# A conv–Mamba–attention hybrid on one core: the scan's exponentials from PSUM to SBUF, with a sibling's other settings

## The chip, the core and the metric

One core of a Trainium2 chip runs the whole program in one launch. The metric is the device time of an execution in microseconds (us). The engines are TensorE (PE in the profile; PEld is its loading of weights), VectorE (DVE), ScalarE (ACT), GpSimd (POOL) and SyncE (SP), which issues nearly all transfers between main memory and SBUF. Matrix products land in PSUM, eight banks of 128 x 512 numbers of 32 bits; GpSimd's operands here are all in SBUF.

## What is computed

The input is x, 8 images of 384 channels x 32 x 32 pixels, all in 32-bit floats. Layer 0 norms each pixel over its channels, runs two selective scans (Mamba) over the 1024 pixels, one in each direction, adds a local branch (a 3x3 depthwise convolution, a sigmoid, times the normed input), and adds all that to x. Layer 1 is causal attention over the 1024 tokens and a feed-forward block whose weights are Kronecker products. What matters here is the scan, cut from the reference:

```python
delta = jax.nn.softplus(jnp.einsum('blr,dr->bld', dt, dt_proj_w) + dt_proj_b)
deltaA = jnp.exp(delta[..., None] * A)
deltaBu = (delta * u)[..., None] * Bm[:, :, None, :]
def step(h, inp):
    dA, dBu, c = inp
    h = dA * h + dBu
    return (h, jnp.einsum('bdn,bn->bd', h, c))
...
y = ys.transpose(1, 0, 2) + u * D_param
y = y * silu(z)
```

There are 384 channels with 16 states each, so 6144 recurrences over 1024 steps, for each image and direction.

## The kernel before

**The scan.** A tile of 128 partitions holds 32 channels x 4 states. For an image the kernel works through four (direction, half) steps of 512 pixels (`STEPS`, line 33), and for each through 12 units: 3 blocks of 128 channels (`cc`) by 4 groups of states (`g`). A unit has four tiles of 128 x 512, handled as a "quad" 128 x 2048. In `scan` (line 974) a unit does this:

- SP has put delta times u, spread over the states, into a quad (`du`, from the pool of five `hs` quads), delta into `dl`, B into `br` and C into `cr`.
- GpSimd multiplies the quad `du` by `br` into the quad `hs` (line 1049); this is B u. The very first quad of the program is done by VectorE in four pieces (line 1047).
- ScalarE takes the exponential of `dl` into `da`, once for each of the four tiles. `da` is a PSUM tile, one of five banks (`DAS`, line 1054).
- VectorE runs `tensor_tensor_scan` on each tile (line 1061): h = da * h + B u. In "split" units the result goes back into `da` (PSUM), ScalarE copies its last column into `carry` if the other half of the image needs it, and VectorE multiplies `da` by `cr` into `hs`, one tile at a time (line 1068). In the other units (`POOL_C`, 4 of 12, and `POOL_END`, 5 of 12, in the last image) the scan's result goes into `hs`, and GpSimd multiplies the whole quad by `cr` (line 1075).
- TensorE sums over the states by four matmuls with `sel` into the one PSUM bank `y`, which also receives the D term (`ud` by `ddiag`, once for both directions of a half, their sum made by GpSimd in `prepare`, line 904) and, for the second direction, the first one's result (`y_t`).

Of the eight PSUM banks `y` has one, `da` five, and all other products ("side work") share two, `w`. At the very end of the program side work gets `da` banks in turn with `w` (`FREE`).

**The side work.** Arrival and norm (`norm_in`), gate (`raw_gate`), the convolutions, the rates (`prepare`), the local branch (`local`, line 832), the projection (`project`, 1103), attention (1152) and the feed-forward block (1269) of an image run beside the scans of that image, the one before or the one after. `local` adds x on GpSimd; `feed_forward` multiplies the normed tokens by `c2` on GpSimd and sums groups on VectorE (`xr`). All weights stay in SBUF from the start on.

**What sets the order.** No loop issues instructions directly. `Plan` records every operation with a due time in units of the scan, written by hand in tables (`FIRST`, `OTHERS`, `LAYER1`, `SCAN`, ...) and spread over the pieces of a stage. `Plan.order` (line 301) then plays all engines with a cost for each operation, binds tiles to buffers, and fixes each engine's queue. Each engine runs its queue in that order, and an instruction waits for the data and buffers it needs. The planner also puts filler matmuls into TensorE's idle time (`y<-zero,ident` in the profile). All operations are issued on line 460, so the profile is read by tile names, not by lines.

Of the kernel before, what the change touches and what calls it, by code (L numbers as in the profile page):

```python
# [30 lines left out]
P = 128  # L31
HB = 512
# [3 lines left out]
TMP, SIDE = 5, 4  # L36
REPS = 4
RUSH = 3.54
START, LATER = -40.0, -8.0
# [3 lines left out]
FIRST = (1.62, 3.96, 10.3, 14.48, 18.18, 21.76)  # L43
SECOND = (22.86, 0.54)
OTHERS = (4.13, 9.04, 14.9, 17.86, 22.66, 25.08, 29.09, 34.25, 42.87, 49.8)
BURST = 8.07
PROJECT = 1.35
LAYER1 = (39.85, 51.29, 60.87, 72.21, 83.5)
LAYER1_6 = (43.34, 50.01, 57.44, 69.38, 72.99)
LAYER1_7 = (39.84, 42.87, 51.35, 57.52, 62.56, 71.14, 71.63, 74.06, 81.9)  # L50
HASTE = 26.32
FREE = ["w", "da", "w", "da"]
EXPS = -0.17
SCAN = (-1.49, -1.1, -0.44, -0.43, -0.36, 0.14, 0.08, 1.19, 0.79)
DU_AHEAD = 3.37
DL_AHEAD = 3.22
DLS = 5
DAS = 5
# [22 lines left out]
class Plan:  # L81
# [9 lines left out]
    LOOSE = ("w", "tmp", "side")  # L91
    HURRY = 8.29
    PATIENCE = 1.77
    TAIL = dict(tensor=0.21, vector=0.117, scalar=0.14, gpsimd=0.1, sync=0.1)
    RAW = 0.07
    NEXT = 0.01
    TURN = 0.1
# [5 lines left out]
    KEEP = 0.65  # L103
# [197 lines left out]
    def order(self):  # L301
# [73 lines left out]
        while issued < total:  # L375
            best = None
            for e in engines:
                ts = [(at(op), op) for op in cand[e]]
                ts = [(t, op) for t, op in ts if t is not None]
                if not ts:  # L380
                    continue
                now = max(clock[e], min(t for t, _ in ts))
                if best is None or now < best[0]:
                    best = (now, e, ts)
# [3 lines left out]
            op = min((op for t, op in ts if t <= now), key=lambda op: op.rank)  # L388
# [14 lines left out]
            if e == "tensor" and self.nothing and now > clock[e]:  # L403

                y = [name for name in left_y if name in self.slot and users[name]]
                begun = bool(y) and left_y[y[0]] not in (0, all_y[y[0]])
                if begun or not y and max([last[n] for n in left_y if n in last], default=0.0) < clock[e]:
                    made = self._fill(max(array) + self.TURN * (form != (P, P)), now, begun)
                    started += made
                    if made:  # L410
                        array = [self.ran[-1][1]] * 4
                        form = P, P
                        now = max(now, array[0] + self.TURN * (op.form != form))
# [50 lines left out]
def conv_attn_kernel(  # L464
# [44 lines left out]
    ps_b = ctx.enter_context(tc.tile_pool(name="ps_b", bufs=1, space=bass.MemoryType.PSUM))  # L509
# [3 lines left out]
    rota = ["w"]  # L513

    def bank():
        rota.append(rota.pop(0))
        if rota[-1] == "w":
            return plan.tile(ps_w, [P, HB], "w", 8 - 1 - DAS)
        return plan.tile(ps_b, [P, HB], "da", DAS)

# [30 lines left out]
    win = load(in_wT[:, :C].rearrange("(cc p) e -> p cc e", p=P), [P, NC, C], "win")  # L551
# [25 lines left out]
    taps, flat = (plan.tile(l0, [P, HB], "side", SIDE)[: C // BC, :P] for _ in range(2))  # L577
# [21 lines left out]
    none = plan.tile(l0, [P, HB], "side", SIDE)[:, : NC * (WP + 1)]  # L599
# [13 lines left out]
    whose = plan.tile(l0, [P, HB], "side", SIDE)[:CG, :P]  # L613
# [23 lines left out]
    for cc in range(NC):  # L637
# [17 lines left out]
        plan.tile(l0, [P, HB], "side", SIDE)[: C // BC, : KW * KW * BC] for _ in range(2)  # L655
# [21 lines left out]
    wz = load(in_wT[:, C:].rearrange("(cc p) e -> p cc e", p=P), [P, NC, C], "wz")  # L677
    wout = load(out_wT.rearrange("(cc p) e -> p cc e", p=P), [P, NC, C], "wout")
    wvs = load(wv.rearrange("(cc p) e -> p cc e", p=P), [P, NC, C], "wvs")

    fc1s = weight([P, NF, P], "fc1s")
    for to in range(NG):
        for g in range(NG):
            plan.sync.dma_start(
                fc1s[to * NJ : (to + 1) * NJ, g::NG], fc1[g * NJ : (g + 1) * NJ]
            )
    fc1f = fc1s.rearrange("p f e -> p (f e)")
    plan.gpsimd.tensor_scalar_mul(fc1f, fc1f, 1.0 / NG)
# [20 lines left out]
    every = weight([P, NJ], "every")  # L709
    plan.vector.tensor_add(every, ident[:, :NJ], ident[:, NJ : 2 * NJ])  # L710
    for g in range(2, NG):
        plan.vector.tensor_add(every, every, ident[:, g * NJ : (g + 1) * NJ])
    emat = weight([P, NJ, NI], "emat")
    plan.vector.tensor_mul(
        emat,
        every.unsqueeze(2).to_broadcast([P, NJ, NI]),
        cp2.unsqueeze(1).to_broadcast([P, NJ, NI]),
    )
    emat = emat.rearrange("p j i -> p (j i)")
    plan.tile(ps_y, [P, HB], "y")  # L720
# [18 lines left out]
    def norm_in(b, h):  # L739
        xt = load_x(b, h)  # L740
        yield
# [36 lines left out]
    def raw_gate(b, h):  # L778

        xn, z = xn_t[b, h], plan.tile(dram, [P, NC, HB], "zr", 4)  # L780
# [51 lines left out]
    def local(b, h):  # L832

        cols = slice(h * HB, (h + 1) * HB)
# [4 lines left out]
        for cc in range(NC):  # L839
            xt = tmp()  # L840
            plan.sync.dma_start(xt, xv[b, :, cc, cols])
# [5 lines left out]
            plan.gpsimd.tensor_add(xt, xt, sg[:, cc])  # L847
            plan.sync.dma_start(lx[cc * P : (cc + 1) * P], xt)
# [55 lines left out]
    def prepare(b, steps):  # L904
# [45 lines left out]
        ud = ud_t[b, steps[0]] = plan.tile(dram, [C, HB], "ud", 4)  # L950
        for cc in range(NC):
            u = uc_t[b, steps[0]][:, cc]
            for si in steps[1:]:
                both = tmp()
                plan.gpsimd.tensor_add(both, u, uc_t[b, si][:, cc])
                u = both
            plan.sync.dma_start(ud[cc * P : (cc + 1) * P], u)
# [13 lines left out]
    def side():  # L971
        return plan.tile(l0, [P, HB], "side", SIDE)

    def scan(b, si, lo=0, hi=HB):
# [5 lines left out]
        ud = ud_t.get((b, si))  # L980
# [25 lines left out]
        for k in range(n_u):  # L1006
            cc, g = divmod(k, SG)
            t = t0 + f * k
            if g == 0:
# [19 lines left out]
                parts = []  # L1029
                if ud is not None:  # L1030
                    parts.append((ddiag[:, cc], ud[cc * P : (cc + 1) * P, lo:hi]))
# [6 lines left out]
                y = plan.tile(ps_y, [P, HB], "y")[:, :n]  # L1038
# [12 lines left out]
            for i in range(NQ):  # L1051
                j = cc * NQ + i
                plan.due, plan.rush = t + f * SCAN[1 + i], EXPS
                da = plan.tile(ps_b, [P, HB], "da", DAS)[:, :n]
                plan.scalar.activation(da, dl[i], AF.Exp, scale=nega[:, j, g : g + 1])
                plan.due, plan.rush = t + f * SCAN[5] * i, 0.0
                o, a, r = hs[:, i], da, da if split else hs[:, i]
                if d:
                    o, a, r = o[:, ::-1], a[:, ::-1], r[:, ::-1]
                init = carry[:, k, i : i + 1] if restore or lo else 0.0  # L1060
                plan.vector.tensor_tensor_scan(r, a, o, init, ALU.mult, ALU.add)
                if split:
                    if save:
                        plan.due, plan.rush = t + f * SCAN[5] * (i + 0.1), RUSH
                        plan.scalar.copy(carry[:, k, i : i + 1], da[:, 0:1] if d else da[:, n - 1 :])
                        plan.rush = 0.0
                    plan.due = t + f * (SCAN[5] * i + SCAN[6])
                    plan.vector.tensor_mul(hs[:, i], da, cr[g])
            if not split:
                if save:  # L1070
                    plan.due, plan.rush = t + f * 0.6, RUSH
                    plan.scalar.copy(carry[:, k], hs[:, :, 0 if d else n - 1])
                    plan.rush = 0.0
                plan.due = t + f * SCAN[8]
                plan.gpsimd.tensor_mul(hs, hs, cr[g].unsqueeze(1).to_broadcast([P, NQ, n]))
# [27 lines left out]
    def project(b, h, t1, lo=0, hi=HB):  # L1103

        yz = [yz_t[b, h, lo, cc] for cc in range(NC)]
        lx = []
        for cc in range(NC):
            lx.append(tmp()[:, : hi - lo])
            plan.sync.dma_start(lx[cc], lx_t[b, h][cc * P : (cc + 1) * P, lo:hi])
        yield  # L1110
        for i in range((hi - lo) // P):
# [7 lines left out]
            for cc in range(NC):  # L1119
                plan.tensor.matmul(  # L1120
                    po[:, cc * P : (cc + 1) * P], lx[cc][:, cols], ident,
                    start=False, stop=cc == NC - 1, is_transpose=True, skip_group_check=True,
                )
# [4 lines left out]
    def token_norm(t1, ti0, nt):  # L1128
# [9 lines left out]
        plan.gpsimd.tensor_scalar_mul(nrm[:, 1], mv[:, :, 0], -1.0)  # L1138
        plan.gpsimd.tensor_mul(nrm[:, 1], nrm[:, 1], nrm[:, 0])
# [12 lines left out]
    def attention(b, t1, t0, n, end=False):  # L1152
# [15 lines left out]
        for i in range(nt):  # L1168
            xt = normed(t1, tile0, nrm, i)
            pt = bank()  # L1170
            for cc in range(NC):
                plan.tensor.transpose(
                    pt[:, cc * P : (cc + 1) * P], xt[:, cc * P : (cc + 1) * P], ident
                )
            plan.scalar.copy(
# [18 lines left out]

        kp = turned(wks, "kp")
# [73 lines left out]
    def feed_forward(b, t1, t0, n, direct=False):  # L1269
# [4 lines left out]
        xr = plan.tile(l1, [P, NT, NJ], "xr")  # L1274
        for i in range(nt):
            xt = normed(t1, tile0, nrm, i).rearrange("p (j i) -> p j i", i=NI)
            plan.gpsimd.tensor_mul(xt, xt, c2.unsqueeze(1).to_broadcast([P, NJ, NI]))
            plan.vector.reduce_sum(xr[:, i], xt, axis=AX.X)
            yield
        px = bank()[:, :n]  # L1280
        for i in range(nt):
            for g in range(NG):
                plan.tensor.matmul(
                    px[g * NJ : (g + 1) * NJ, i * P : (i + 1) * P], xr[:, i], ident,
                    start=True, stop=True, skip_group_check=True,
# [6 lines left out]
        for f0 in range(0, NF, NF // 2):  # L1292
            gl = plan.tile(l1, [P, NF // 2, HB], "gl")[:, :, :n]
            for k in range(0, NF // 2, 2):
                ph = [bank()[:, :n], bank()[:, :n]]
                for i in range(2):
                    plan.tensor.matmul(ph[i], fc1s[:, f0 + k + i], xrT, start=True, stop=True)
# [10 lines left out]
            po = bank()[:, :n]  # L1308
            for k in range(NF // 2):
# [3 lines left out]
                    start=k < NG, stop=k >= NF // 2 - NG, skip_group_check=True,  # L1313
                )
            if f0 == 0:
                plan.scalar.copy(ob, po)
            else:
                plan.vector.tensor_add(ob, po, ob)
# [41 lines left out]
    for b in range(NB):  # L1360
# [21 lines left out]
        else:  # L1382
            first, rate = SECOND if b == 1 else (B - PER, 1.0)
            v = [first + rate * u for u in OTHERS]
# [12 lines left out]
        for si, (d, h) in enumerate(STEPS):  # L1397

            parts = ((0, HQ), (HQ, HB)) if last and si == 3 else ((0, HB),)
            for lo, hi in parts:  # L1400
                e = B + (si + hi / HB) * NU * SG
                scan(b, si, lo, hi)
                if si >= 2:
                    rota[:] = FREE if last and si == 3 and hi == HB else ["w"]
# [93 lines left out]
```

## Time and profile before

| | us |
|---|---|
| median of 3 runs | 3051.7 (3050.02 to 3054.4) |
| the profiled execution, its own time | 3053.55 |
| its span, first to last instruction | 3051.8 |
| TensorE / VectorE / ScalarE / GpSimd busy | 2698.0 / 2700.1 / 2175.5 / 2686.7 |
| mean granted TensorE clock | 0.969 of full |
| moved by DMA | 632.77 MB, mean 207 GB/s |

Everything below is read from one profiled execution. A group is all instructions of one engine with the same output and inputs by name ("hs<-da,cr" is hs written from da and cr); with it come the count, the busy time, the mean duration of one, and the time the engine sat idle just before, with what it waited for. An instruction's duration includes its start-up, so instructions back to back start closer together than one lasts.

### The profile page before, as it was taken

What the parts mean: (1) busy time and instruction counts of PE and PEld (TensorE: products, weight loads), DVE (VectorE), ACT (ScalarE), POOL (GpSimd) and SP (SyncE); (2) the same over time, 40 slices, a digit from 0 to 9 for tenths busy, and PEclk for the clock granted to TensorE, in tenths of its full rate; (3) what the DMA queues carried; (4) which work ended last, traced back from release to release, by engine and by line L of the source; (5) the groups of instructions that cost most, each with busy time, mean ns of one, the idle gap of its engine ahead of it and who ended that gap; (6) DMA issues with size and microseconds to landing.
All of it is one profiled execution on the core that took longest, in us unless ns stands there. A gap on an engine that the chain in (4) does not pass through costs nothing. (4 is left out here: it accounts for less than half of the span.)

```text
span 3051.8 us, 39365 instructions
## 1 busy us (share of the span) xinstructions
PE 2698.0 (88%) x12021; PEld 1188.4 (39%) x12021; DVE 2700.1 (88%) x3514; ACT 2175.5 (71%) x3928; POOL 2686.7 (88%) x914
## 2 busy tenths in 40 slices
PE   8877897998999899988889898999989998988889
PEld 3322343343443434333343434434343433434445
DVE  3898938998899989998999979999899989999982
ACT  3765656778778786867768686787868687676774
POOL 2999868989898999989898999989998999999960
PEclk9988998999999999999999999999999999999999
DMA  7786776567766677666766667556775577533410
GB/s 249 242 275 215 230 263 221 183 225 251 240 202 200 221 259 229 201 205 223 244 194 204 225 217 251 198 193 224 258 231 186 201 242 254 168 131 121 149 54 17
DMA packets 345836, 632.77 MB, mean 207 GB/s; under 512 B 42544, under 2 KB 57208, under 8 KB 345624
## 3 DMA queue, kind: packets, MB, share of 16 engines
q1 hardware_dynamic: 345496, 630.14, 62.5%
q8 instruction: 95, 1.56, 0.2%
q14 instruction: 117, 0.96, 0.1%
q0 software_dynamic: 128, 0.11, 0.0%
HBM read 475.71 MB, written 154.38 MB: 206 GB/s over the span
## 5 line engine op out<-in xcount | busy, mean ns | idle before, releaser
L460 POOL TENSOR_TENSOR hs<-hs,br 128x2048 f32<-128x2048 f32 (+1 forms) x395 | 1739.0, 4418 | 167.8 <-PE y L460 85.2
L460 ACT ACTIVATE da<-dl,nega 128x512 f32<-128x512 f32 (+1 forms) x1584 | 1036.3, 676 | 402.5 <-DVE hs L460 386.4
L460 DVE TENSOR_TENSOR hs<-da,cr 128x512 f32<-128x512 f32 (+1 forms) x1036 | 656.8, 666 | 27.7 <-ACT carry L460 27.0
L460 DVE TENSOR_TENSOR_SCAN da<-da,carry,hs 128x512 f32<-128x512 f32 (+1 forms) x532 | 628.4, 1220 | 38.9 <-POOL hs L460 24.7
L460 DVE TENSOR_TENSOR_SCAN da<-da,hs 128x512 f32<-128x512 f32 x504 | 598.0, 1218 | 64.9 <-ACT da L460 48.4
L460 POOL TENSOR_TENSOR hs<-hs,cr 128x2048 f32<-128x2048 f32 (+1 forms) x137 | 600.1, 4380 | 54.4 <-DVE hs L460 31.4
L460 PE MATMUL y<-hs,sel 128*32 128x512 f32 (+1 forms) x3168 | 467.9, 616 | 97.3 <-POOL hs L460 81.1
L460 PE MATMUL y<-zero,ident 128*128 128x256 f32 x1470 | 387.9, 397 | 0.0
L460 DVE TENSOR_TENSOR_SCAN hs<-da,carry,hs 128x512 f32<-128x512 f32 (+1 forms) x284 | 324.1, 1192 | 13.0 <-ACT da L460 7.7
L460 PEld LDWEIGHTS y<-zero,ident 128*128 128x128 f32 x1470 | 271.2, 195 | 149.3 <-issue 119.1
L460 DVE TENSOR_TENSOR_SCAN hs<-da,hs 128x512 f32<-128x512 f32 x264 | 308.3, 1208 | 20.4 <-ACT da L460 19.4
L460 PEld LDWEIGHTS y<-hs,sel 128*32 128x32 f32 x3168 | 93.4, 111 | 337.7 <-issue 128.5
L458 ACT ACT_TABLE_LOAD x164 | 210.4, 1283 | 2.9
L460 PE MATMUL w<-q,fc1s 128*128 128x512 f32 (+1 forms) x396 | 198.2, 617 | 15.0 <-ACT gl L460 7.4
L460 PE MATMUL w<-v,p 128*128 128x384 f32 x562 | 200.8, 504 | 8.4 <-ACT p L460 4.7
L460 ACT COPY carry<-da 128x1 f32<-128x1 f32 x532 | 81.0, 163 | 170.8 <-DVE da L460 168.8
L460 PE MATMUL w<-rep,cit 96*32 96x512 f32 x1152 | 153.0, 606 | 9.4 <-DMA rep<-xq 7.3
L460 ACT COPY gl<-w 128x512 f32<-128x512 f32 (+2 forms) x254 | 137.5, 551 | 12.8 <-PE w L460 11.7
L460 PE MATMUL w<-wout,side 128*128 128x384 f32 x378 | 137.9, 503 | 7.9 <-ACT t L460 3.6
L460 PEld LDWEIGHTS w<-v,p 128*128 128x128 f32 x562 | 105.1, 194 | 90.9 <-ACT p L460 19.7
L460 PE MATMUL w<-xn,wz 128*128 128x512 f32 x288 | 132.8, 601 | 3.9 <-ACT tmp L460 3.4
L460 PE MATMUL w<-xn,win 128*128 128x512 f32 x288 | 130.7, 600 | 1.9 <-ACT tmp L460 0.9
(188 smaller groups left out, 3421.2 us busy)
## 6 DMA issues: line engine op xcount, KB each, us to landing
dl<-dd SPq DMA_DIRECT2D x372, 256.0 KB, 4.0
hs<-db SPq DMA_DIRECT2D x372, 256.0 KB, 4.5
rep<-up SPq DMA_DIRECT2D x180, 257.5 KB, 4.3
rep<-xq SPq DMA_DIRECT2D x192, 222.4 KB, 4.9
br<-bd SPq DMA_DIRECT2D x124, 256.0 KB, 4.6
cr<-bd SPq DMA_DIRECT2D x124, 256.0 KB, 4.3
tmp<-in_x_dram SPq DMA_DIRECT2D x96, 256.0 KB, 4.6
dd<-tmp SPq DMA_DIRECT2D x96, 256.0 KB, 3.4
```

Of the source, the lines that this page charges most:

```text
L458: self.nc.scalar.preload_act_table_set(table)
L460: op.call(*args, **{k: self._bind(v) for k, v in op.kw.items()})
```

## The change

- **da in SBUF.** `da` becomes seven SBUF tiles. PSUM is split anew: six banks for side work, two for `y`. The rotation of side work into `da` banks goes.
- **Scans.** Every scan writes over B u in the quad `hs`. `carry` is copied once per quad. In split units VectorE multiplies the whole quad by `cr` at once (128 x 2048). Which units are split stays.
- **The sibling's other settings.** `tmp` and `side` become one pool of eight. The four large weights share two SBUF tiles (`heavy`) and are loaded again for each image (`wvs` for each attention part). The D term is added for each direction, without GpSimd's sum. `local` no longer adds x; `project` adds it by a second transposing matmul. `nrm` is finished by one VectorE instruction instead of two of GpSimd. The feed-forward block transposes the normed tokens and applies `c2` by a matmul (`c2s`) instead of GpSimd and VectorE; `fc1s` is a quarter of the size, used by 32 rows at a time; the second half's sum into `ob` is a matmul.
- **Planner.** Other due times, per image in part; a limit on how far ahead of the oldest candidate an operation may be taken (`SIGHT`); a penalty for a switch of ScalarE's table (`YIELD`).

```diff
-TMP, SIDE = 5, 4
+TMP = 8
+YS = 2
+WTS = 2
-DAS = 5
+DAS = 7
...
     def bank():
-        rota.append(rota.pop(0))
-        if rota[-1] == "w":
-            return plan.tile(ps_w, [P, HB], "w", 8 - 1 - DAS)
-        return plan.tile(ps_b, [P, HB], "da", DAS)
+        return plan.tile(ps_w, [P, HB], "w", 8 - YS)
...
+    def heavy(nm, key):
+        if (nm, key) not in big:
+            src = dict(win=in_wT[:, :C], wz=in_wT[:, C:], wout=out_wT, wvs=wv)[nm]
+            t = big[nm, key] = plan.tile(const, [P, NC, C], "wt", WTS)
+            plan.sync.dma_start(t, src.rearrange("(cc p) e -> p cc e", p=P))
+        return big[nm, key]
...
-            plan.gpsimd.tensor_add(xt, xt, sg[:, cc])
-            plan.sync.dma_start(lx[cc * P : (cc + 1) * P], xt)
+            plan.sync.dma_start(lx[cc * P : (cc + 1) * P], sg[:, cc])
...
-        ud = ud_t[b, steps[0]] = plan.tile(dram, [C, HB], "ud", 4)
-        for cc in range(NC):
-            u = uc_t[b, steps[0]][:, cc]
-            for si in steps[1:]:
-                both = tmp()
-                plan.gpsimd.tensor_add(both, u, uc_t[b, si][:, cc])
-                u = both
-            plan.sync.dma_start(ud[cc * P : (cc + 1) * P], u)
+        for si in steps:
+            ud = ud_t[b, si] = plan.tile(dram, [C, HB], "ud", 8)
+            for cc in range(NC):
+                plan.sync.dma_start(ud[cc * P : (cc + 1) * P], uc_t[b, si][:, cc])
...
-                y = plan.tile(ps_y, [P, HB], "y")[:, :n]
+                y = plan.tile(ps_y, [P, HB], "y", YS)[:, :n]
...
-                da = plan.tile(ps_b, [P, HB], "da", DAS)[:, :n]
+                da = plan.tile(l0, [P, HB], "da", DAS)[:, :n]
                 plan.scalar.activation(da, dl[i], AF.Exp, scale=nega[:, j, g : g + 1])
                 plan.due, plan.rush = t + f * SCAN[5] * i, 0.0
-                o, a, r = hs[:, i], da, da if split else hs[:, i]
+                o, a = hs[:, i], da
                 if d:
-                    o, a, r = o[:, ::-1], a[:, ::-1], r[:, ::-1]
+                    o, a = o[:, ::-1], a[:, ::-1]
                 init = carry[:, k, i : i + 1] if restore or lo else 0.0
-                plan.vector.tensor_tensor_scan(r, a, o, init, ALU.mult, ALU.add)
-                if split:
-                    if save:
-                        plan.due, plan.rush = t + f * SCAN[5] * (i + 0.1), RUSH
-                        plan.scalar.copy(carry[:, k, i : i + 1], da[:, 0:1] if d else da[:, n - 1 :])
-                        plan.rush = 0.0
-                    plan.due = t + f * (SCAN[5] * i + SCAN[6])
-                    plan.vector.tensor_mul(hs[:, i], da, cr[g])
-            if not split:
-                if save:
-                    plan.due, plan.rush = t + f * 0.6, RUSH
-                    plan.scalar.copy(carry[:, k], hs[:, :, 0 if d else n - 1])
-                    plan.rush = 0.0
-                plan.due = t + f * SCAN[8]
-                plan.gpsimd.tensor_mul(hs, hs, cr[g].unsqueeze(1).to_broadcast([P, NQ, n]))
+                plan.vector.tensor_tensor_scan(o, a, o, init, ALU.mult, ALU.add)
+            if save:
+                plan.due, plan.rush = t + f * (3 * SCAN[5] + SCAN[6]), RUSH
+                plan.scalar.copy(carry[:, k], hs[:, :, 0 if d else n - 1])
+                plan.rush = 0.0
+            plan.due = t + f * (3 * SCAN[5] + SCAN[6] + 0.01 if split else SCAN[8])
+            eng = plan.vector if split else plan.gpsimd
+            eng.tensor_mul(hs, hs, cr[g].unsqueeze(1).to_broadcast([P, NQ, n]))
...
-            for cc in range(NC):
-                plan.tensor.matmul(
-                    po[:, cc * P : (cc + 1) * P], lx[cc][:, cols], ident,
-                    start=False, stop=cc == NC - 1, is_transpose=True, skip_group_check=True,
-                )
+            for cc in range(NC):
+                for k in range(2):
+                    plan.tensor.matmul(
+                        po[:, cc * P : (cc + 1) * P], lx[cc][k][:, cols], ident, start=False,
+                        stop=cc == NC - 1 and k == 1, is_transpose=True, skip_group_check=True,
+                    )
...
-        plan.gpsimd.tensor_scalar_mul(nrm[:, 1], mv[:, :, 0], -1.0)
-        plan.gpsimd.tensor_mul(nrm[:, 1], nrm[:, 1], nrm[:, 0])
+        plan.vector.scalar_tensor_tensor(
+            nrm[:, 1], mv[:, :, 0], -1.0, nrm[:, 0], ALU.mult, ALU.mult
+        )
...
-            xt = normed(t1, tile0, nrm, i).rearrange("p (j i) -> p j i", i=NI)
-            plan.gpsimd.tensor_mul(xt, xt, c2.unsqueeze(1).to_broadcast([P, NJ, NI]))
-            plan.vector.reduce_sum(xr[:, i], xt, axis=AX.X)
+            xt = normed(t1, tile0, nrm, i)
+            pt = bank()
+            for cc in range(NC):
+                plan.tensor.transpose(
+                    pt[:, cc * P : (cc + 1) * P], xt[:, cc * P : (cc + 1) * P], ident
+                )
+            plan.scalar.copy(
+                xT[:, :, i * P : (i + 1) * P],
+                pt[:, :C].rearrange("p (cc t) -> p cc t", cc=NC),
+            )
...
+                    px[g * NJ : (g + 1) * NJ], c2s[:, cc], xT[:, cc],
+                    start=cc == 0, stop=cc == NC - 1, skip_group_check=True,
...
+            if f0:
+                plan.tensor.matmul(po, ident, ob, start=True, stop=False, skip_group_check=True)
...
-            if f0 == 0:
-                plan.scalar.copy(ob, po)
-            else:
-                plan.vector.tensor_add(ob, po, ob)
+            plan.scalar.copy(ob, po)
```

## The prediction

> **What bounds the kernel now.** I read the page's busy shares first, then the groups of instructions with shapes kept apart, then the waits of VectorE and GpSimd, the busy time by stretches, and last the timeline of the first scans.
>
> The first view, the page's busy line:
>
> ```profile
> PE 2698.0 (88%) x12021; PEld 1188.4 (39%) x12021; DVE 2700.1 (88%) x3514; ACT 2175.5 (71%) x3928; POOL 2686.7 (88%) x914
> ```
>
> TensorE, VectorE (DVE) and GpSimd (POOL) are each busy for 88% of the 3051.8 us span. 388 us of TensorE's are filler (y<-zero,ident, 1470 passes), so the pair to watch is VectorE and GpSimd: the kernel is as short as it is because these two work at the same time. If they had to take turns, their 2700 and 2687 us would add up to 5387.
>
> The second view is the groups by shape: what the two do in the scan (busy us and mean ns of one behind the bar).
>
> ```profile
> L460 DVE TENSOR_TENSOR hs<-da,cr 128x512 f32<-128x512 f32 x980 | 635.2, 680 | 27.6 <-ACT carry L460 27.0
> L460 DVE TENSOR_TENSOR_SCAN da<-da,hs 128x512 f32<-128x512 f32 x504 | 598.0, 1218 | 64.9 <-ACT da L460 48.4 <-POOL hs L460 12.1 <-issue 4.3
> L460 DVE TENSOR_TENSOR_SCAN hs<-da,carry,hs 128x512 f32<-128x512 f32 x244 | 296.6, 1267 | 10.9 <-ACT da L460 5.6 <-POOL hs L460 5.3
> ...
> L460 POOL TENSOR_TENSOR hs<-hs,br 128x2048 f32<-128x2048 f32 x371 | 1682.7, 4550 | 162.8 <-PE y L460 80.3 <-DMA zr<-tmp 47.5 <-DMA out_dram<-tmp 7.0
> L460 POOL TENSOR_TENSOR hs<-hs,cr 128x2048 f32<-128x2048 f32 x127 | 576.3, 4538 | 47.7 <-DVE hs L460 24.7 <-ACT carry L460 10.9 <-DMA out_dram<-tmp 10.7
> ```
>
> In every one of these VectorE rows one input, da, lies in PSUM and only the other in SBUF. So VectorE takes 1.22 us for a scan and 0.68 us for a multiply although GpSimd is multiplying beside it nearly all the time.
>
> The third view is what decides the prediction. Once, at the very start, VectorE multiplies two SBUF tiles (hs by br, first quad of the first scan). The four are one group, minimum/median/maximum in ns:
>
> ```profile
> L460 DVE TENSOR_TENSOR hs<-hs,br x4: 675/686/4987, 57.2 to 61.6; 128x512 f32<-128x512 f32 x4
> ```
>
> And the timeline of VectorE and of GpSimd there (start us, us):
>
> ```profile
> 60.42 6.17 DVE L460 TENSOR_TENSOR hs<-hs,br 128x512 f32<-128x512 f32 x3
> 66.52 1.22 DVE L460 TENSOR_TENSOR_SCAN da<-da,hs 128x512 f32<-128x512 f32 x1
> ```
>
> ```profile
> 61.20 4.84 POOL L460 TENSOR_TENSOR hs<-hs,br 128x2048 f32<-128x2048 f32 x1 [47.49 <-DMA zr<-tmp]
> ```
>
> Three of the four take 0.68 us. The last starts at 61.6, when a GpSimd multiply has run since 61.20, and ends at 66.6: 4.99 us. GpSimd ended at 66.04, 0.55 before, and multiplies issued back to back are 0.58 apart (two in 1.27 at 1509.38, one alone 0.69). So it did nothing until GpSimd was done, and then ran at its usual speed. GpSimd's own 4.84 are 0.29 over its mean of 4.55: the VectorE multiply before it, begun around 61.0, was still running. The scan at 66.52, with da in PSUM, runs in 1.22. Nowhere else in this trace does VectorE read two large SBUF tiles beside a busy GpSimd.
>
> The Trainium skill's "SBUF — State Buffer", section "Who interferes with whom", says why: VectorE's second SBUF input comes through a read interface that GpSimd uses too, and whichever starts first holds it for its whole instruction, while the other is blocked. The multiply's 4.99 us agrees. The rule names no operation and so takes in the scans, which the row does not show; with it all 1584 scans exclude GpSimd (the forecast's sum), and by the row alone only the 259 multiplies would (the first rival's). It speaks against this change.
>
> **The change part by part.** Counts are from the two programs' instruction orders.
>
> 1. *Exponentials to SBUF.* ScalarE writes da into one of seven SBUF tiles. The 1584 scans stay, but each now reads two SBUF tiles (da and hs). Alone their cost stands: back to back they are 1.12 us apart without a carry (three in 3.46 at 70.11) and 1.18 with one (four in 4.80 at 1521.85). 768 x 1.12 + 720 x 1.18 + 96 half-width ones at about 0.63 (their 0.73 less 0.1 of overlap) = 1770 us. What a wait would add is the unknown. Per scan: from 0 (the scans of before, PSUM beside GpSimd) to 4.31 (4.99 less 0.68, the one blocked multiply). A gain is small: scans that write to SBUF take 1.208 against 1.218 into PSUM, so 0.01 for an operand moved, 16 us in all, left out. I take the row's end, as it is the only one with two SBUF inputs.
>
> 2. *One multiply by C per quad.* 1036 multiplies go (980 x 0.59 + 56 x 0.32 apart, about 596 us); 259 of 128x2048 come. No row has that width on VectorE; from 256 (413 ns) to 512 (680 ns) a column costs 1.04 ns, so 0.58 + 1536 x 1.04 ns = 2.18 us; 245 of these and 14 half ones at 1.11 make 550 us. Saved: 46 us. These read two SBUF tiles too.
>
> 3. *Other VectorE work.* xr<-xt goes (34.0), as does the sum into p (about 11); 34 tiny nrm come (about 3). VectorE becomes 2700 - 46 - 42, about **2610 us**, of which 1770 + 550 = 2320 have two SBUF inputs and 290 do not.
>
> 4. *GpSimd.* The multiplies hs by br (395) and by cr (137) stay at 1739 + 600. tmp<-tmp,uc (60.6), xt by row_sb (57.1), tmp<-uc,uc (56.2), both nrm (14.8) and fc1s (4.1) go: 2687 - 193 = **2494 us**, all of it reading SBUF.
>
> 5. *TensorE, ScalarE, DMA.* TensorE gains 48 ddiag matmuls (0.54 us each, 26), some 195 transposes of xt and 192 of x (0.17 each, 67), 204 for c2s (0.29, like cp1s, 60) and 17 sums for ob (10), and loses xr (27) and 86 fillers (45): about +90, to 2790. ScalarE loses 532 carry copies (81) and gains 133 (26), 64 transposes' evictions (30) and 19 copies to p (11): -14. SP issues 2566 transfers for 2448 (118 at some 0.55 us, 65 us of its queue, beside the rest), and 41 weight loads of 590 KB add 24 MB to 633. All of this lies beside the VectorE/GpSimd pair and is costed at nothing; without that cover TensorE's +90 is the largest. Six banks for side work and two for y, instead of two and one, can remove at most the waits they end: GpSimd's 85 us for y, and VectorE's 18.
>
> **The sum (forecast).** If the pair can't overlap while VectorE reads two SBUF tiles: 2610 + 2494 = 5104. GpSimd may run under VectorE's other 290 us; I take half, -145 (0 to -290). Head and tail hold neither:
>
> ```profile
> 0.00:57.00 57.00, 50.88 (x143) 23.03 (x144) 12.92 (x56) 19.24 (x25) 6.12 (x15) 1.00 0.72 233
> ...
> 2963.00:3052.00 89.00, 80.83 (x390) 48.34 (x386) 20.15 (x55) 41.95 (x92) 4.81 (x10) 1.00 0.06 21
> ```
>
> (columns: length, PE, PEld, VectorE, ScalarE, GpSimd, clock, DMA). Of 146 us the two work 44, so +102. Sum 5061. To this comes time when both wait for something else: 0 at the low end; at the high end the 365 us that GpSimd idles now. Half of its waits are for y or the scans' output, which last no longer than now while the other side works; I take 40, a tenth of it. **5100 us.** Profiled time is 3053.55 for a span of 3051.8, and the median 3051.7, so no correction is due. Bounds: low 5104 - 290 + 102 = 4916, less up to 0.4 us for each of 673 GpSimd instructions if VectorE may run beside their start and end (the 0.29 and 0.55 above leave little): 4650. High: 5061 + 145 + 365, about 5570.
>
> **Rivals.**
> - *Only the multiply excludes, the scan does not* (a scan passes an element in 2.1 ns against the multiply's 1.04, and might fetch both inputs in turn). For: no row shows a scan with two SBUF inputs. Against: nothing shows such a fetch. Each of 259 multiplies then finds GpSimd busy 8 times in 10 and waits half of 4.55: 1.8 us, 470 in all. VectorE: 2610 + 470 + 352 idle as now = 3430. GpSimd waits for them in turn but has its 365 us of slack. **3400 us** (3100 with idle time gone).
> - *Faster: the two share their access to SBUF element by element, and the 4.99 us belong to GpSimd's first multiply alone.* Place: every scan. For: it was GpSimd's first tensor instruction, and there is one such row. Against: it ended just when GpSimd's did, and GpSimd's cost there was normal. Price: VectorE 2610 at before's ratio of span to busy (3052/2700 = 1.13) gives **2950 us**. It decides only if the mean delay of the 1843 VectorE instructions stays under (3052 - 2950)/1843 = 0.055 us.
> - *The change doesn't do it* (da still in PSUM): excluded, the built program has all scans hs<-da,hs and da in the SBUF pool.
>
> **How the numbers follow.** Forecast 0.86; multiply alone 0.06; shared access 0.07; the last 0.01 is for landing within 0.2%, about what a measurement of this kernel can tell from no change. Slower 0.92, same 0.01, faster 0.07. Of the forecast's cases about 95 in 100 lie between 4650 and 5600, that is 0.82 in all, so the range need not reach 3400.
>
> **What will show it.** Right: scans of 2 to 3 us in the mean with a minimum still near 1.18 and a maximum near 5.7; GpSimd's hs<-hs,br rising above 4.55 too; in any mid-kernel slice VectorE's and GpSimd's time overlapping only on paper, inside waits; TensorE's share falling to about 55%. Step 2 is right if the shortest 128x2048 multiply is 2.2 to 2.3 us; steps 3 to 5 if counts and shortest durations stand and no other engine ends long waits. Wrong: scans at 1.2 us throughout (the second rival), or scans at 1.2 and only multiplies at up to 6.7 (the first).

## The result and the profile after

| | before | after |
|---|---|---|
| median, us | 3051.42 (3050.02 to 3054.4, 4 runs) | 5014.77 (5013.79 to 5015.86, 4 runs) |
| span of the profiled execution, us | 3051.8 | 5011.8 |
| VectorE / GpSimd busy, us | 2700 / 2687 | 4760 / 3025 |

The ratio is 1.6432, 95% interval 1.6404 to 1.6461: the change makes the kernel 64% slower. The forecast was 5100 us, the range 4650 to 5600.

The busy line and the row of TensorE's granted clock (tenths, 40 slices) on the page of the changed kernel:

```profile
PE 3060.0 (61%) x12262; PEld 1305.0 (26%) x12262; DVE 4759.5 (95%) x2692; ACT 2200.3 (44%) x3610; POOL 3024.8 (60%) x688
...
PEclk8768777787777777787777777777777777777789
```

VectorE went from 88% busy to 95% and has 822 instructions fewer: it spends the added time inside its instructions, not between them. GpSimd has 226 fewer and is busy 338 us longer, but it also stands idle for 1987 us, where it was 365. Its longest waits are for TensorE's sums into y, which free a quad, and those wait longest for VectorE (1096 us). The groups of VectorE by shape, costliest first:

```profile
L489 DVE TENSOR_TENSOR_SCAN hs<-da,hs 128x512 f32<-128x512 f32 x768 | 1851.1, 2464 | 43.0 <-ACT da L489 26.1 <-POOL hs L489 16.8
L489 DVE TENSOR_TENSOR_SCAN hs<-da,carry,hs 128x512 f32<-128x512 f32 x720 | 1790.4, 2540 | 22.9 <-POOL hs L489 19.3 <-ACT da L489 3.6
L489 DVE TENSOR_TENSOR hs<-hs,cr 128x2048 f32<-128x2048 f32 x245 | 737.0, 3008 | 10.3 <-ACT carry L489 9.6
...
L489 DVE BATCH_NORM_STATS2 st<-t 128x6 f32<-128x384 f32 x128 | 67.1, 542 | 8.6 <-ACT t L489 8.4
```

A scan went from 1.2 to 2.5 us in the mean, while the statistics, with one SBUF input, stay at 0.54 (0.55 before). The spread by tile names, whatever the shape (minimum/median/maximum, ns), says how:

```profile
L489 DVE TENSOR_TENSOR_SCAN hs<-da,hs x768: 1166/1211/5612, 60.3 to 4751.8; 128x512 f32<-128x512 f32 x192
L489 DVE TENSOR_TENSOR hs<-hs,cr x259: 1192/2274/6558, 81.6 to 4911.2; 128x2048 f32<-128x2048 f32 x123, 128x1024 f32<-128x1024 f32 x7
```

More than half of the scans take 1.2 us as ever. The longest hold a whole GpSimd multiply: 5.6 is 1.2 and 4.4. In the trace 436 scans last over 3 us, and each of them ends 1.08 to 1.09 us after a GpSimd instruction. GpSimd's own groups:

```profile
L489 POOL TENSOR_TENSOR hs<-hs,br 128x2048 f32<-128x2048 f32 x371 | 1983.1, 5355 | 791.1 <-PE y L489 532.1 <-issue 77.0 <-DMA hs<-db 73.1
L489 POOL TENSOR_TENSOR hs<-hs,cr 128x2048 f32<-128x2048 f32 x127 | 652.3, 5136 | 857.3 <-DVE hs L489 377.3 <-ACT carry L489 368.4 <-DVE sm L489 55.6
```

4.55 us became 5.36, 0.8 more; a scan by itself takes 1.2. The timelines of VectorE and then of GpSimd in mid-kernel show the turns being taken (start us, us):

```profile
2534.66 5.51 DVE L489 TENSOR_TENSOR_SCAN hs<-da,hs 128x512 f32<-128x512 f32 x1
...
2540.09 5.50 DVE L489 TENSOR_TENSOR_SCAN hs<-da,hs 128x512 f32<-128x512 f32 x1
```

```profile
2534.07 5.02 POOL L489 TENSOR_TENSOR hs<-hs,br 128x2048 f32<-128x2048 f32 x1 [14.86 <-PE y L489]
...
2539.05 5.45 POOL L489 TENSOR_TENSOR hs<-hs,br 128x2048 f32<-128x2048 f32 x1
```

The scan begun at 2534.66 ends at 2540.17, 1.1 us after GpSimd's multiply (2539.09), so nearly all its own time lies behind that. The next multiply, begun at 2539.05, ends at 2544.50; it took 0.9 longer than 4.55, about the time in which that scan ran. The next scan waits for it in turn and ends 1.1 us after it.

### The profile page after: what moved, and what is told of

Its sections match the earlier page's. It is cut to its first block, busy times and chain, and to the rows that moved or that the text cites. A ratio compares the mean times of both kernels' runs of the same rounds, so it can differ in the third digit from the quotient of the medians.

```text
span 5011.8 us, 38650 instructions
## 1 busy us (share of the span) xinstructions
PE 3060.0 (61%) x12262; PEld 1305.0 (26%) x12262; DVE 4759.5 (95%) x2692; ACT 2200.3 (44%) x3610; POOL 3024.8 (60%) x688
## 5 line engine op out<-in xcount | busy, mean ns | idle before, releaser
L489 POOL TENSOR_TENSOR hs<-hs,br 128x2048 f32<-128x2048 f32 (+1 forms) x395 | 2049.2, 5198 | 804.1 <-PE y L489 539.7
L489 DVE TENSOR_TENSOR_SCAN hs<-da,carry,hs 128x512 f32<-128x512 f32 (+1 forms) x816 | 1905.2, 2388 | 25.1 <-POOL hs L489 19.3
L489 DVE TENSOR_TENSOR_SCAN hs<-da,hs 128x512 f32<-128x512 f32 x768 | 1851.1, 2464 | 43.0 <-ACT da L489 26.1
L489 DVE TENSOR_TENSOR hs<-hs,cr 128x2048 f32<-128x2048 f32 (+1 forms) x259 | 756.2, 2920 | 10.3 <-ACT carry L489 9.6
L489 PE MATMUL w<-xn,wt 128*128 128x512 f32 x576 | 303.9, 675 | 21.6 <-DVE xn L489 19.8
L489 POOL TENSOR_TENSOR uc<-uc,tmp 128x512 f32<-128x512 f32 x93 | 199.5, 2176 | 89.6 <-ACT tmp L489 89.6
L489 ACT COPY gl<-w 128x384 f32<-128x384 f32 (+2 forms) x318 | 158.5, 530 | 65.1 <-PE w L489 64.6
L489 PEld LDWEIGHTS w<-xn,wt 128*128 128x128 f32 x576 | 119.8, 218 | 201.2 <-issue 158.2
L489 PE MATMUL w<-wt,tmp 128*128 128x384 f32 x384 | 144.2, 515 | 5.9 <-DVE tmp L489 5.9
L489 PE MATMUL w<-q,fc1s 32*128 32x512 f32 (+1 forms) x408 | 142.7, 765 | 6.7 <-ACT uc L489 4.8
```

Source lines behind the costliest of these rows:

```text
L489: op.call(*args, **{k: self._bind(v) for k, v in op.kw.items()})
```

## The experiments

Theory: a VectorE instruction with two SBUF inputs, scans included, and a GpSimd instruction that reads SBUF exclude each other. Rivals: only the plain multiply excludes; SBUF inputs are slow by themselves; the sibling's other settings, the new order or TensorE's clock cost the time.

**1. The disputed cost by itself (m_port).** One stretch of VectorE instructions after another, each but the first beside six of GpSimd's; in short:

```python
scans("scansbalone", va[:, :N])                       # va, vb: SBUF
scans("scanpsmul", pa);          pool("mul")          # pa: PSUM
scans("scansbmul", va[:, :N]);   pool("mul")
scans("scansbset", va[:, :N]);   pool("set")
scans("scansbone", va[:, :N]);   pool("one")
...                                                   # multiplies, copies, reductions beside pool("mul")
```

> A kernel that leaves out all of the computation and writes a constant: stretches in which VectorE runs one kind of instruction while GpSimd runs six of its own over 128x2048. Theory (an instruction of VectorE with two SBUF inputs and a GpSimd instruction that reads SBUF exclude each other, scans too): 18 scans with one input in PSUM beside six GpSimd multiplies take 20 us and nobody waits; 18 scans with both in SBUF and the six multiplies take turns, 18 x 1.12 + 6 x 4.5 = 47 us together; beside GpSimd memsets, which read nothing, the scans keep their 1.12; beside a one-input GpSimd multiply they take turns again; ten 128x2048 and thirty 128x512 VectorE multiplies take turns too, 49 and 44 us; reductions of one SBUF tile don't wait. Rival (only the plain multiply excludes, a scan doesn't): the 18 scans with both in SBUF take 20 us beside the multiplies. Rival (an SBUF tile is a slow input for a scan by itself): the 18 scans are slow with GpSimd idle as well.

The groups of VectorE; the first part of a name is the instruction, the last what GpSimd does meanwhile:

```profile
L564 DVE TENSOR_TENSOR multwidemul<-va,vb 128x2048 f32<-128x2048 f32 x10 | 48.1, 4810 | 0.3
L548 DVE TENSOR_TENSOR_SCAN scansbmul<-va,vb 128x512 f32<-128x512 f32 x18 | 46.8, 2601 | 0.6
L569 DVE TENSOR_TENSOR multmul<-va,vb 128x512 f32<-128x512 f32 x30 | 45.9, 1530 | 1.0
L574 DVE COPY copymul<-va 128x512 f32<-128x512 f32 x40 | 42.2, 1056 | 1.3
L548 DVE TENSOR_TENSOR_SCAN scansbone<-va,vb 128x512 f32<-128x512 f32 x18 | 41.6, 2314 | 0.6
L548 DVE TENSOR_TENSOR_SCAN scansbset<-va,vb 128x512 f32<-128x512 f32 x18 | 22.0, 1224 | 0.6
L548 DVE TENSOR_TENSOR_SCAN scansbalone<-va,vb 128x512 f32<-128x512 f32 x18 | 22.0, 1224 | 0.6
L548 DVE TENSOR_TENSOR_SCAN scanpsmul<-pa,vb 128x512 f32<-128x512 f32 x18 | 22.0, 1223 | 0.6
L579 DVE TENSOR_REDUCE redmul<-va 128x1 f32<-128x512 f32 x30 | 20.6, 686 | 1.0
```

The run was made once. The scan with two SBUF inputs takes 1.224 us alone and 1.223 with one of them in PSUM: SBUF is not slow by itself, and that rival falls. Beside multiplies the 18 last 46.8 us, expected 47: VectorE's and GpSimd's times add up. Beside fills, which read nothing, they keep 1.224; beside GpSimd multiplies with a single input they wait again. The wide and the narrow multiplies take 48.1 and 45.9 us, 49 and 44 expected. Reductions don't wait. The scan excludes, and what it excludes is GpSimd's reading. Timelines of GpSimd for the PSUM and the SBUF stretch give the other side:

```profile
36.97 27.37 POOL L538 TENSOR_TENSOR gc<-ga,gb 128x2048 f32<-128x2048 f32 x6
...
66.03 31.33 POOL L538 TENSOR_TENSOR gc<-ga,gb 128x2048 f32<-128x2048 f32 x6
```

Six multiplies lose 4 us, 0.8 for each of five scans between them: the two take turns one for one, and as GpSimd's instruction is nearly four times as long, VectorE does most of the waiting.

**2. Only the scans back to PSUM (e_psum).**

```diff
-YS = 2
+YS = 1
...
-DAS = 7
+DAS = 4
...
-        return plan.tile(ps_w, [P, HB], "w", 8 - YS)
+        return plan.tile(ps_w, [P, HB], "w", 8 - YS - DAS)
...
-                da = plan.tile(l0, [P, HB], "da", DAS)[:, :n]
+                da = plan.tile(ps_b, [P, HB], "da", DAS)[:, :n]
```

> The changed kernel with da back in PSUM (four banks, three for side work, one for y); scans still write over B u and VectorE still multiplies the quad by C from SBUF. So of VectorE's instructions with two SBUF inputs the 1584 scans are gone and the 259 multiplies stay. Theory: the sum of the first rival of the prediction, 3400 us (3100 to 3450). Rival (the sibling's other settings, the planner's new order or TensorE's lower clock cost the time): above 4500 us.

Measured: 3578.25 us, ratio 1.170 (1.1659 to 1.1742). From 5015 it falls by 1437: the scans' share, together with the split of PSUM that goes with it. It is 128 us above the theory's range. In the profiled execution VectorE stands idle for 463 us, where the sum had 352; runs 3 and 6, which have four banks for da too, idle 453 and 448. So the lost bank is the likely cause of the miss; it was not tried in this kernel. Its VectorE groups:

```profile
L489 DVE TENSOR_TENSOR hs<-hs,cr 128x2048 f32<-128x2048 f32 x245 | 1011.2, 4128 | 19.5 <-ACT carry L489 18.8
L489 DVE TENSOR_TENSOR_SCAN hs<-da,hs 128x512 f32<-128x512 f32 x768 | 882.5, 1199 | 82.0 <-ACT da L489 54.6 <-POOL hs L489 21.6 <-POOL uc L489 4.9
L489 DVE TENSOR_TENSOR_SCAN hs<-da,carry,hs 128x512 f32<-128x512 f32 x720 | 873.2, 1261 | 86.4 <-ACT da L489 47.6 <-POOL hs L489 38.4 <-DMA db<-uc 0.2
```

The scans are back at 1.2 us and the wide multiplies still wait, longer than with the scans in SBUF (3.01): 4.13 us, 1.86 over their own 2.27.

**3. The scan of before with all the other settings (e_rest).** The split of PSUM as in run 2, and in `scan` the lines of before: split units scan into `da` and multiply tile by tile.

```diff
-                plan.vector.tensor_tensor_scan(o, a, o, init, ALU.mult, ALU.add)
+                plan.vector.tensor_tensor_scan(r, a, o, init, ALU.mult, ALU.add)
...
+                    plan.vector.tensor_mul(hs[:, i], da, cr[g])
```

> The changed kernel with the scan of before: da in PSUM (four banks, three for side work, one for y), split units scan into da and multiply tile by tile from PSUM; all the sibling's other settings stay. Theory: no VectorE instruction of weight has two SBUF inputs; VectorE 2700 - 42 = 2660 us busy, GpSimd 2494; near before, 2900 to 3150 us. Rival (the other settings cost the time): above 3500 us.

Measured: 3165.9 us, ratio 1.0363 (1.0346 to 1.038), 16 us over the range. So 412 us of run 2 come with the wide multiplies from SBUF (VectorE is 421 us less busy here), and the other settings with this split of PSUM cost 114 over before, not 1960. Its busy line:

```profile
PE 2802.1 (88%) x12642; PEld 1258.6 (40%) x12642; DVE 2713.8 (86%) x3469; ACT 2224.9 (70%) x4017; POOL 2504.1 (79%) x688
```

GpSimd has its 2504 us (2494 were reckoned), 183 less than before, and the kernel is no shorter for it.

**4. GpSimd's scan multiplies to VectorE (e_alldve).**

```diff
-                plan.gpsimd.tensor_mul(hs, du, br[g].unsqueeze(1).to_broadcast([P, NQ, n]))
+                plan.vector.tensor_mul(hs, du, br[g].unsqueeze(1).to_broadcast([P, NQ, n]))
...
-            eng = plan.vector if split else plan.gpsimd
+            eng = plan.vector
```

> The changed kernel with GpSimd's scan multiplies (395 by B, 137 by C) moved to VectorE, everything else as changed. Theory: VectorE's own work grows from 2610 to 2610 + 835 + 290 = 3735 us, but nobody holds it up any more except GpSimd's 141 short multiplies; with some 250 us of idle time about 4000 us (3850 to 4200), so a thousand less than the changed kernel although VectorE does a thousand more. Rival (a scan is slow with da in SBUF whatever GpSimd does): 4760 us of VectorE now plus 1125, near 5900 us.

Measured: 4008.61 us (one run), as the theory had it (about 4000). The page's busy line, and below it the group of scans without a carry:

```profile
PE 3191.6 (80%) x13772; PEld 1499.7 (37%) x13772; DVE 3860.0 (96%) x3224; ACT 2241.0 (56%) x3618; POOL 338.7 (8%) x156
```

```profile
L489 DVE TENSOR_TENSOR_SCAN hs<-da,hs 128x512 f32<-128x512 f32 x768 | 932.7, 1255 | 0.0
```

VectorE does 532 multiplies more and the kernel is 1006 us shorter than the changed one. With exclusion, GpSimd's help costs more (4.55 us a quad) than doing it on VectorE (2.27). It is still 31% over before.

**5. GpSimd without reading (e_memset).** The kernel leaves out the products with B, and in part those with C.

```diff
-                plan.gpsimd.tensor_mul(hs, du, br[g].unsqueeze(1).to_broadcast([P, NQ, n]))
+                plan.gpsimd.memset(hs, 0.0)
...
-            eng.tensor_mul(hs, hs, cr[g].unsqueeze(1).to_broadcast([P, NQ, n]))
+            if split:
+                eng.tensor_mul(hs, hs, cr[g].unsqueeze(1).to_broadcast([P, NQ, n]))
+            else:
+                eng.memset(hs, 0.0)
```

> The changed kernel in which GpSimd fills the quads with zeros where it multiplied (395 by B, 137 by C); it leaves out B, so all scans run on zeros. GpSimd works in the same places but reads nothing. Theory (only GpSimd's reads exclude VectorE): VectorE keeps its own 2610 us plus some 300 idle, 2850 to 3050 us, with scans at 1.2 us in the mean, apart from waits for GpSimd's 141 short multiplies. Rival (any GpSimd instruction excludes): 532 fills of 1.80 us, 930 us, and 171 us of multiplies come on top of VectorE's 2610: 3700 to 4000 us, with scans well above 1.2 us in the mean.

Measured: 3094.53 us (one run), 45 over the theory's range, 600 under the rival's. Groups of VectorE, and GpSimd's fills:

```profile
L489 DVE TENSOR_TENSOR_SCAN hs<-da,hs 128x512 f32<-128x512 f32 x768 | 954.9, 1297 | 40.6 <-ACT da L489 34.0 <-POOL hs L489 6.5
...
L489 DVE TENSOR_TENSOR hs<-hs,cr 128x2048 f32<-128x2048 f32 x245 | 575.6, 2350 | 38.7 <-ACT carry L489 38.2
```

```profile
L489 POOL MEMSET hs<- 128x2048 f32 x498 | 888.7, 1805 | 1459.8 <-PE y L489 709.3 <-DVE hs L489 310.4 <-ACT carry L489 157.7
```

With 532 GpSimd instructions in the same places, but reading nothing, the scans take 1.30 us; no scan lasts over 2.31 us here, and a short GpSimd multiply takes 1.2 to 1.3 by itself, so what is left is taken as waits for the 141 of those. With them VectorE is busy 2724 us, not 2610, and it idles 369, where some 300 were expected: that is the miss. This is nearly the changed kernel without its exclusion, with GpSimd's load lightened besides, and it is not faster than before.

**6. The split of PSUM alone (e_bank4), and 7. two of the other settings alone (e_less_pool).**

```diff
-DAS = 5
+DAS = 4
```

> The kernel before with four PSUM banks for da and three for side work, instead of five and two; nothing else. The run that kept the scan of before with all the sibling's other settings took 3.6% longer than before; it had this split too. If the split is what cost it, this takes 3100 to 3170 us; if the other settings and their due times cost it, within 1% of before, 3020 to 3085 us.

Measured: 3146.18 us, ratio 1.0316 (1.0298 to 1.0334), within the range for the split. So one bank fewer for da and one more for side work cost 94 us in the kernel before. Run 3's 114 are likely the same loss for the most part, as VectorE idles alike there (453 us, here 448, before 352).

```diff
-            plan.gpsimd.tensor_add(xt, xt, sg[:, cc])
-            plan.sync.dma_start(lx[cc * P : (cc + 1) * P], xt)
+            plan.sync.dma_start(lx[cc * P : (cc + 1) * P], sg[:, cc])
...
-                both = tmp()
-                plan.gpsimd.tensor_add(both, u, uc_t[b, si][:, cc])
```

> The kernel before with two of the sibling's other settings alone: x is added in the projection by TensorE, and the D term is added for each direction, so GpSimd loses 93 additions, 117 us, and TensorE gains 59. If GpSimd's load bounds the kernel before, it takes 2960 to 3030 us; if the hand-written due times bind more than the load, it doesn't gain, 3040 to 3120 us.

Measured: 3103.95 us, ratio 1.018 (1.0159 to 1.0201). GpSimd is busy 2575 us instead of 2687, and the kernel is 1.8% longer, in the range for due times that bind. The waits that grew most in this run, VectorE's and then GpSimd's:

```profile
DVE side L460 <- PE y L460: 50.0, 15, 9.5
```

```profile
POOL nrm L460 <- DVE mv L460: 115.8, 9, 43.6
...
POOL hs L460 <- DVE hs L460: 73.7, 20, 12.4
```

(columns: us in total, times, longest; before: 18.0, 82.5 and 31.4). The time freed on GpSimd is spent waiting. That an order laid out for the old load is the cause is inferred from these waits; a new set of due times was not tried.

No version here beats the kernel before.

## Why the prediction was right

- **The row it rested on.** One multiply of 4.99 us, once in 3514 instructions, was the only place where the old kernel did what the new one does all the time. Runs 1, 2, 4 and 5 each show that it was no accident of the first GpSimd instruction. That the old trace holds it at all was luck of timing: in run 6 all four of these multiplies take 0.67 to 0.69 us.
- **Step 1, the scans.** That a scan excludes like a multiply was taken from one row of another operation. Run 1 shows it (1.224 to 2.60 us), and run 2 prices it: 1437 us.
- **Step 2, the multiplies.** 2.18 us apart was reckoned, so 2.28 for one alone; the shortest is 2.26, the median 2.27.
- **Steps 3 and 4.** Own work of 2610 and 2494 us was reckoned. GpSimd's is 2504 where nothing of weight makes it wait (run 3). VectorE's comes out at 2601 us in the changed kernel and 2605 in run 5, if each group's stretched instructions are counted at the length of its unstretched ones. One entry was missed: the 34 small nrm, put at 3 us, read two SBUF tiles too, and 30 of them take 37 us (0.16 in the median, 4.39 at most). The traffic grew by 45 MB, not 24; run 7's two settings alone add 24.
- **Step 5.** "Costed at nothing" held for the time, but not TensorE's 2790: it is 3060 with the clock at 0.77 (below), and 2802 in run 3 at 0.96. TensorE's share was to be 55% and is 61%. VectorE's longest waits for TensorE are 24 and 20 us in all, too little for the lower clock to cost the time. Runs 2 to 5, which change what VectorE and GpSimd do and, in 2 and 3, the split of PSUM, bring the time back and the clock with it (0.89 to 0.96).
- **The sum.** It is 85 us over the measured time. The terms, against the measured ones on the reckoned bases: VectorE waits 4760 - 2610 = 2150 us inside its instructions, GpSimd 3025 - 2494 = 531. So 2494 - 2150 = 344 of GpSimd's work ran without holding VectorE up, not 145: this term was mis-sized. In the trace GpSimd is busy for 111 us beside VectorE's instructions with at most one SBUF input, and for 81 under VectorE's idle time, which the sum had left out. The other 150 or so are taken to lie at starts and ends, where the two overlap a little (a scan that waited ends 1.08 us after GpSimd and takes 1.20 alone); the prediction had that in its low bound only. In return VectorE idles 252 us, of which the stretches of the changed kernel show 121 in head and tail and 131 between:

```profile
0.00:57.00 57.00, 50.29 (x152) 24.55 (x153) 11.98 (x55) 19.23 (x25) 6.08 (x15) 1.00 0.66 209
57.00:4920.00 4863.00, 2925.06 (x11677) 1229.90 (x11676) 4732.03 (x2590) 2140.05 (x3490) 3018.70 (x673) 0.76 0.42 136
4920.00:5012.00 92.00, 84.67 (x437) 50.58 (x435) 15.53 (x47) 41.01 (x96) 0.00 (x0) 1.00 0.08 27
```

  (columns: length, PE, PEld, VectorE, ScalarE, GpSimd, clock, DMA.) Put as the prediction did, 2610 + 2494 - 344 + 252 = 5012: 199 us more overlap than reckoned, against 110 us more idle time than the 102 + 40. The mechanism carries the sum; that these two misses have opposite signs, and leave 85 us, is luck. Either alone would have stayed in the range.
- **First rival** (only the multiply excludes, 3400). Run 2 is that case on the chip: 3578. The wait per multiply was put at 1.8 us and is 1.86; what the rival's sum lacked is mostly idle time, 463 us instead of 352. The rival itself falls with run 1.
- **Second rival** (shared access, faster, 2950). It falls with run 1. Its price stays untested: run 5 has little exclusion left and takes 3095 us, but about 120 of its VectorE's 2724 us are still waits. Its ratio of span to busy time is 1.135, close to the 1.13 that the price took from before; in run 3 it is 1.17.

The shares, in a ladder from the runs: before 3052; da in four banks 3146; the other settings 3166; wide multiplies from SBUF 3578; scans from SBUF 5015. The steps hold in this order, and the last one also takes da out of PSUM and splits the banks anew; from other ends they may differ, as taking turns depends on both engines' load.

The Trainium skill's "SBUF — State Buffer", section "Who interferes with whom", says that a VectorE instruction with two SBUF inputs contends with a GpSimd instruction that reads SBUF, not with one that only writes it. The runs agree: 2.60 us for a scan beside multiplies, 1.224 beside fills. It also says that an instruction with at most one SBUF input stays clear unless it runs in a mode that uses two ports, and that copies can enter such modes. Run 1 agrees: reductions take at most 0.687 us beside multiplies, while copies of 32-bit numbers, which have one input, take 1.06 in the mean, 0.42 at the shortest and 4.74 at the longest; that these ran in such a mode is not shown by itself.

## What to carry to other kernels

Before moving an operand from PSUM to SBUF, ask whether it leaves a VectorE instruction with two SBUF inputs while GpSimd reads SBUF: if so, add the two engines' times instead of taking the larger. Look in the old trace for a single instruction that already has the new form, and read its maximum, not its mean. Where the two must exclude each other, GpSimd's share is worth moving to VectorE, if its instruction takes GpSimd longer than VectorE.

## What the runs showed of the hardware that was not expected

- **Turns are not always one for one.** In run 2 one wide multiply lasted 19.38 us; it sat behind GpSimd instructions that followed each other without letting it in. VectorE's and GpSimd's timelines:

```profile
962.47 19.38 DVE L489 TENSOR_TENSOR hs<-hs,cr 128x2048 f32<-128x2048 f32 x1
```

```profile
960.66 4.51 POOL L489 TENSOR_TENSOR hs<-hs,cr 128x2048 f32<-128x2048 f32 x1
965.13 8.98 POOL L489 TENSOR_TENSOR hs<-hs,br 128x2048 f32<-128x2048 f32 x2
974.07 1.17 POOL L489 TENSOR_TENSOR uc<-uc,rep 128x512 f32<-128x512 f32 x1
975.20 4.49 POOL L489 TENSOR_TENSOR hs<-hs,br 128x2048 f32<-128x2048 f32 x1
```

  Five in a row, each at its usual length, and the multiply ends 2.2 us after the last. Three of 259 multiplies lasted over 8 us. It goes the other way too: the changed kernel's first GpSimd multiply lasted 8.26 us (59.88 to 68.14), behind five VectorE instructions in a row, the last of which ended at 63.82. What decides this was not settled.
- **TensorE's granted clock fell from 0.97 to 0.77** in the changed kernel, with about the same work (2% more matmuls) stretched over 64% more time; y<-hs,sel went from 616 to 777 ns. It stayed at 1.00 in the head and tail, where TensorE is busy 88% and 92% of the time, and is 0.76 between, at 60%.
